# The last stage of a two-layer graph kernel: x1 of half of the rows added by TensorE into held PSUM tiles

## The chip, the cores and the metric

The kernel runs on one core of one Trainium2 chip. The metric is device time in microseconds (us), measured on the core. The kernel before takes 2655.48 us (median of three runs, 2652.28 to 2655.86). Its profiled execution has a span of 2651.3 us, and all moments given below are microseconds from the start of that span.

## What is computed

The input `x` has 16 images of 1024 rows and 256 channels, in float32. Layer 0 is a graph step with attention, a residual and a layer norm over the channels; it gives x1. Layer 1 aggregates x1 over a normalised adjacency matrix, then runs two linear layers, each followed by a batch norm over all 16 x 1024 rows, then adds x1 and takes a layer norm. Cut to the end of layer 1, with which this case deals:

```python
h   = relu(_batchnorm(x @ W1.T + b1, g1, be1))    # 512 features
out = _batchnorm(h @ W2.T + b2, g2, be2)          # 256 features
# and outside
x = _layernorm(x1 + out, axis=-1)                 # (x - mean) / sqrt(var + 1e-5)
```

The second batch norm needs the statistics of all 16 images before the first value of the result can be finished. So there is a point in the kernel at which everything waits for the last product of `h @ W2.T`, and a last stage behind it that passes over all images once more.

## The kernel before

The kernel is hand-scheduled: inside `tc.manual_schedule` TensorE (PE), ScalarE (ACT) and VectorE (DVE) each run their instructions in the order that the program writes them, apart from small moves that put an instruction ahead of another that would wait. GpSimd (POOL) computes small coefficient columns. All bulk transfers of the stage are issued from SyncE's queue (SP), in order.

The second linear layer (L1456) keeps its result transposed: for each image `b` a tile `o2T[b]` of 128 partitions with two halves `c` of 128 features, each with all 1024 rows in the free dimension. VectorE moves each half from PSUM with the bias added (L1460) and takes its batch norm statistics (L1464). All 16 `o2T` tiles stay in SBUF. After the last image `coefficients2` aggregates the statistics of a half (L1227), and GpSimd works out a scale `sg2` and a shift `sh2` for each feature (L1228 to L1231).

The last stage then runs, for each image:

- `scale_shift(b)`: two ACT passes of 128x1024, one for each half, that apply `sg2` and `sh2` in place (L1485).
- `residual2(b)`: TensorE turns `o2T[b]` back to rows, four 128x128 transposes into each of four PSUM tiles of 512 columns, one for each pair of row blocks (L1497). VectorE adds each PSUM tile to x1, which lies in SBUF as `xf[b]`, in place (L1502), and takes layer norm statistics of each 128x256 block, eight for an image (L1504). Ten small GpSimd operations turn these into `rstd` and `nmr`, the scale and the shift of each row (L1510 to L1519).
- `finish(b)`: eight ACT passes of 128x256 that write the normalised rows over `o2T[b]` (L1526), the store of the image (L1530), and the load of x1 for image `b + 7` (L1428) into the buffer that is now free. The x1 of the first three images is loaded while the linear layer still runs, that of the next four at the start of the stage.

The order in which these are written is `residual2(b)`, `scale_shift(b + 1)`, `finish(b - 1)`: on ACT the two passes for the next image stand ahead of the eight for the image before. The four PSUM tiles of an image come from two pools of two buffers.

Image 0's scale-and-shift for a half waits for that half's coefficients, and the second half's are the last to come.

Of the kernel before, what the change touches and what calls it, by code (L numbers as in the profile page):

```python
# [515 lines left out]
def fast_path(  # L516
# [34 lines left out]
    def open_psum():  # L551

        stack = ExitStack()
        for tag in "sto":
            psum[tag] = stack.enter_context(tc.tile_pool(name=f"ps_{tag}", bufs=2, space=PSUM))
        return stack
# [3 lines left out]
    def tile_s(name):  # L560
        return psum["s"].tile([P, N], F32, tag="s", name=name)

    def tile_t(name):
        return psum["t"].tile([P, HALF], F32, tag="t", name=name)

    def tile_o(name):
        return psum["o"].tile([P, HALF], F32, tag="o", name=name)
# [7 lines left out]
    ident = const.tile([P, P], F32, name="ident")  # L575
# [95 lines left out]
    H0, H1 = slice(0, HALF), slice(HALF, N)  # L671
# [3 lines left out]
    cols = {}  # L675
# [24 lines left out]
    with (  # L700
# [10 lines left out]
        st = {}  # L711
# [404 lines left out]
        with tc.manual_schedule(engines={mybir.EngineType.PE, mybir.EngineType.Activation, mybir.EngineType.DVE}):  # L1116
# [48 lines left out]
            for j in range(len(bursts)):  # L1165
                b, u = j // PERB, j % PERB
# [30 lines left out]
            j = len(bursts)  # L1197
# [14 lines left out]


    w1T, w2T = wl["w1T"], wl["w2T"]
    bn1_st = const.tile([P, HC, 2 * B, 6], F32, name="bn1_st")
    bn2_st = const.tile([P, CC, 2 * B, 6], F32, name="bn2_st")

    def batchnorm(stats, gamma, beta, k, name):

# [15 lines left out]
    with (  # L1235
# [9 lines left out]
        def bank(name):  # L1245
            return ps8.tile([P, HALF], F32, tag="bank", name=name)

        def temps(k):
            return lambda key, name: strt.tile([P, HALF], F32, tag=f"{key}{k}", name=f"{key}_{name}")


        wS = strt.tile([P, 4, C], F32, name="wS")
# [133 lines left out]
        def scale_shift1(h, k):  # L1386
            nc.scalar.activation(  # L1387
                h, h, AF.Relu, bias=sh1[:, k : k + 1], scale=sg1[:, k : k + 1]
            )
# [3 lines left out]
        for k in range(HC):  # L1393
            ps = [bank(f"ph_{k}_{half}") for half in range(2)]
            for c in range(CC):
                for half, hs in enumerate((H0, H1)):
                    nc.tensor.matmul(
                        ps[half], w1T[:, c, k * P : (k + 1) * P], t[:, c, hs],
                        start=(c == 0), stop=(c == CC - 1),
# [11 lines left out]
        nc.gpsimd.dma_start(h_d[B - 1], ht)  # L1411

    graph.close()
    ctx.enter_context(open_psum())

# [4 lines left out]
    with tc.tile_pool(name="o2p", bufs=1) as o2p:  # L1420
        o2T = [
            o2p.tile([P, CC, N], F32, tag=f"o2_{b}", name=f"o2_{b}") for b in range(B)
        ]
        xf = {}

        def load_x1(b, pool, tag):
            xf[b] = pool.tile([P, NCH, C], F32, tag=tag, name=f"xf_{b}")
            nc.sync.dma_start(xf[b], x1_d[b])  # L1428

        coefficients2, sg2, sh2 = batchnorm(bn2_st, cols["g2"], cols["be2"], CC, "bn2")  # L1430
        with (
            tc.tile_pool(name="hl", bufs=2) as hl,
            tc.manual_schedule(
                engines={mybir.EngineType.PE, mybir.EngineType.Activation, mybir.EngineType.DVE}
            ),
        ):
            hs_of = {0: h0}

            def load_h(b):
                ht = hl.tile([P, HC, N], F32, tag="hl", name=f"hl_{b}")  # L1440
                nc.sync.dma_start(ht, h_d[b])
                hs_of[b] = [ht[:, k, :] for k in range(HC)]

            load_h(1)
            for b in range(B):
                if b + 2 < B:
                    load_h(b + 2)
                if b + 1 < B:
                    for k in range(HC):
                        scale_shift1(hs_of[b + 1][k], k)  # L1450
                h = hs_of.pop(b)
                for c in range(CC):
                    ps = tile_s(f"po2_{b}_{c}")
                    for k in range(HC):
                        for hs in (H0, H1):
                            nc.tensor.matmul(  # L1456
                                ps[:, hs], w2T[:, k, c * P : (c + 1) * P], h[k][:, hs],
                                start=(k == 0), stop=(k == HC - 1),
                            )
                    nc.vector.tensor_scalar(  # L1460
                        o2T[b][:, c, :], ps, cols["b2"][:, c : c + 1], None, ALU.add
                    )
                    for half, hs in enumerate((H0, H1)):
                        nc.vector.bn_stats(bn2_st[:, c, 2 * b + half, :], o2T[b][:, c, hs])  # L1464
                    if b == B - 1:
                        coefficients2(c)
                if b >= B - 3:
                    load_x1(b - (B - 3), xp, "x")

        with (
            tc.tile_pool(name="fin2", bufs=4) as fin2,
            tc.manual_schedule(
                engines={mybir.EngineType.PE, mybir.EngineType.Activation, mybir.EngineType.DVE}
            ),
        ):
            for b in range(3, 7):
                load_x1(b, fin2, "xf")  # L1480

            def scale_shift(b):
                for c in range(CC):
                    o = o2T[b][:, c, :]
                    nc.scalar.activation(  # L1485
                        o, o, AF.Identity, bias=sh2[:, c : c + 1], scale=sg2[:, c : c + 1]
                    )

            def residual2(b):
                xt = xf[b]  # L1490
                st = small.tile([P, NCH, 6], F32, tag="ln_st", name=f"st_l1_{b}")
                for pair in range(NCH // 2):
                    pt = tile_t(f"pf_{b}_{pair}") if pair % 2 else tile_o(f"pf_{b}_{pair}")
                    for j in range(2):
                        n = 2 * pair + j
                        for c in range(CC):
                            nc.tensor.transpose(  # L1497
                                pt[:, j * C + c * P : j * C + (c + 1) * P],
                                o2T[b][:, c, n * P : (n + 1) * P], ident,
                            )  # L1500
                    xs = xt[:, 2 * pair : 2 * pair + 2, :].rearrange("p n c -> p (n c)")
                    nc.vector.tensor_add(xs, pt, xs)  # L1502
                    for n in (2 * pair, 2 * pair + 1):
                        nc.vector.bn_stats(st[:, n, :], xt[:, n, :])  # L1504

                me, qe, mo, qo = (st[:, :, k] for k in (1, 2, 4, 5))
                w = small.tile([P, 4, NCH], F32, tag="ln_w", name=f"w_l1_{b}")
                rstd, nmr, dif, var = (w[:, k, :] for k in range(4))
                pool = nc.gpsimd
                pool.tensor_tensor(nmr, me, mo, ALU.add)  # L1510
                pool.tensor_tensor(dif, me, mo, ALU.subtract)
                pool.tensor_tensor(var, qe, qo, ALU.add)
                pool.tensor_scalar(var, var, 1.0 / C, EPS, ALU.mult, ALU.add)
                pool.tensor_tensor(dif, dif, dif, ALU.mult)
                pool.tensor_scalar(dif, dif, 0.25, None, ALU.mult)
                pool.tensor_tensor(var, var, dif, ALU.add)
                pool.tensor_tensor(rstd, var, mhalf, ALU.pow)
                pool.tensor_tensor(nmr, nmr, rstd, ALU.mult)
                pool.tensor_scalar(nmr, nmr, -0.5, None, ALU.mult)  # L1519
                return rstd, nmr  # L1520

            def finish(b, rstd, nmr):
                xt = xf.pop(b)
                y = o2T[b].rearrange("p c n -> p (c n)").rearrange("p (n c) -> p n c", c=C)
                for n in range(NCH):
                    nc.scalar.activation(  # L1526
                        y[:, n, :], xt[:, n, :], AF.Identity,
                        bias=nmr[:, n : n + 1], scale=rstd[:, n : n + 1],
                    )
                nc.sync.dma_start(out[b].rearrange("(n p) c -> p n c", p=P), y)  # L1530
                if b + 7 < B:
                    load_x1(b + 7, *((fin2, "xf") if 3 <= b < 7 else (xp, "x")))

            scale_shift(0)
            coeffs = {}
            for b in range(B):
                coeffs[b] = residual2(b)
                if b + 1 < B:
                    scale_shift(b + 1)
                if b:  # L1540
                    finish(b - 1, *coeffs.pop(b - 1))
            finish(B - 1, *coeffs.pop(B - 1))


# [41 lines left out]
```

## Time and profile before

| what | value |
|---|---|
| time | 2655.48 us |
| span of the profiled execution | 2651.3 us |
| TensorE busy over the span | 96% |
| last product of the second linear layer | ends at 2531.7 |
| first normalising pass of the last stage | starts at 2549.07 |
| last normalising pass | ends at 2644.28 |
| ACT busy, 2560 to 2580 | 20.00 of 20.00 us |
| VectorE busy in the same stretch | 17.77 |
| TensorE busy in the same stretch, and its granted clock | 11.39, 0.56 |

How to read the profile's lines: a table by stage gives for each stretch its length and then, engine by engine, the busy time and the number of instructions in brackets; PEld is TensorE's loading of weights, which overlaps its products. PEclk is the granted clock of TensorE as a share of full speed, then come the busy share of the 16 DMA engines and what they moved. A line of the timeline has the start, the duration of the merged group, the engine, the source line, the operation, its tiles and shapes and the number of instructions. In square brackets stands how long the engine had been idle before and which instruction ended the wait.

### The profile page before, as it was taken

What the parts mean: (1) busy time and instruction counts of PE and PEld (TensorE: products, weight loads), DVE (VectorE), ACT (ScalarE), POOL (GpSimd) and SP (SyncE); (2) the same over time, 40 slices, a digit from 0 to 9 for tenths busy, and PEclk for the clock granted to TensorE, in tenths of its full rate; (3) what the DMA queues carried; (4) which work ended last, traced back from release to release, by engine and by line L of the source; (5) the groups of instructions that cost most, each with busy time, mean ns of one, the idle gap of its engine ahead of it and who ended that gap; (6) DMA issues with size and microseconds to landing.
All of it is one profiled execution on the core that took longest, in us unless ns stands there. A gap on an engine that the chain in (4) does not pass through costs nothing. (4 is left out here: it accounts for less than half of the span.)

```text
span 2651.3 us, 31994 instructions
## 1 busy us (share of the span) xinstructions
PE 2553.7 (96%) x12966; PEld 1110.1 (42%) x12966; DVE 1600.2 (60%) x2160; ACT 1126.8 (43%) x1349; POOL 336.2 (13%) x407
## 2 busy tenths in 40 slices
PE   8999999999999999999999999999999999999964
PEld 4443444444434434444444343344444444444443
DVE  5465665756656657666566576765655655533376
ACT  5363563654645636545446354410101001233368
POOL 0001000100100011001000100321222211100044
PEclk9999999999999999999999999999999999999975
DMA  4001101001011011010110110112122122353367
GB/s 143 2 9 41 33 10 41 21 22 33 9 41 33 9 41 33 10 41 3 39 33 9 41 49 1 41 64 95 80 95 95 66 92 82 137 202 143 149 222 240
DMA packets 134557, 168.94 MB, mean 64 GB/s; under 512 B 86785, under 2 KB 120065, under 8 KB 124033
## 3 DMA queue, kind: packets, MB, share of 16 engines
q1 hardware_dynamic: 129568, 116.47, 14.2%
q0 software_dynamic: 4832, 50.34, 4.6%
q8 instruction: 103, 1.69, 0.3%
q14 instruction: 54, 0.43, 0.0%
HBM read 99.36 MB, written 67.44 MB: 63 GB/s over the span
## 5 line engine op out<-in xcount | busy, mean ns | idle before, releaser
L908 ACT ACTIVATE p<-ps 128x1024 f32<-128x1024 f32 x512 | 495.7, 1020 | 179.5 <-PE ps L903 142.9
L933 DVE TENSOR_TENSOR acc<-acc,p 128x1024 f32<-128x1024 f32 x384 | 483.2, 1258 | 61.0 <-ACT p L908 32.4
L903 PE MATMUL ps<-qT,kT 64*64 64x512 f32 x4096 | 490.6, 594 | 1.4 <-ACT p L908 1.4
L924 PE MATMUL po<-p,v 64*64 64x512 f32 x4096 | 485.3, 589 | 0.0
L805 PE MATMUL pg<-wg,x 128*128 128x512 f32 x960 | 425.2, 596 | 0.0
L979 POOL TENSOR_TENSOR x<-x,o 128x512 f32<-128x512 f32 x64 | 109.5, 1711 | 1434.8 <-DVE o L974 1434.8
L924 PEld LDWEIGHTS po<-p,v 64*64 64x64 f32 x4096 | 156.7, 133 | 282.8 <-issue 282.6
L805 PEld LDWEIGHTS pg<-wg,x 128*128 128x128 f32 x960 | 177.6, 190 | 226.9 <-issue 203.3
L903 PEld LDWEIGHTS ps<-qT,kT 64*64 64x64 f32 x4096 | 146.1, 132 | 280.2 <-issue 231.5
L817 ACT ACTIVATE qT<-qT 128x512 f32<-128x512 f32 x64 | 40.3, 631 | 482.0 <-DVE qT L814 481.9
L1456 PE MATMUL po<-hl,w12T 128*128 128x512 f32 x512 | 220.3, 592 | 3.1 <-ACT hl L1387 2.3
L814 DVE SCALAR_TENSOR_TENSOR qT<-pg,para_s 128x512 f32<-128x512 f32 x64 | 43.9, 689 | 271.1 <-PE pg L805 269.8
L793 DVE SCALAR_TENSOR_TENSOR wg<-wg,adj_s 128x1024 f32<-128x1024 f32 x128 | 153.1, 1217 | 15.5 <-ACT wg L789 15.5
L784 ACT ACTIVATE wg<-crow,ccol 128x1024 f32<-128x1024 f32 x128 | 146.6, 1146 | 11.8 <-DMA crow<-c 11.8
L1456 PEld LDWEIGHTS po<-hl,w12T 128*128 128x128 f32 x512 | 97.1, 190 | 126.3 <-issue 120.5
L789 ACT ACTIVATE wg<-wg 128x1024 f32<-128x1024 f32 x128 | 135.5, 1060 | 2.6
L1387 ACT ACTIVATE hl<-hl,bn_sh,bn_sg 128x1024 f32<-128x1024 f32 x64 | 74.3, 1229 | 135.0 <-DMA hl<-h 133.6
L855 PE MATMUL pv<-kvw_s,xT 128*128 128x256 f32 x512 | 124.0, 385 | 1.6 <-ACT kT L846 1.6
L1460 DVE TENSOR_SCALAR o<-po,col_b 128x1024 f32<-128x1024 f32 x32 | 41.1, 1284 | 139.1 <-PE po L1456 139.1
L842 PE MATMUL pk<-xT,kvw_s 128*128 128x512 f32 x256 | 120.3, 592 | 0.0
L855 PEld LDWEIGHTS pv<-kvw_s,xT 128*128 128x128 f32 x512 | 94.9, 190 | 51.9 <-issue 27.6
L1286 PE MATMUL a_agg<-ahT,x1l 128*128 128x512 f32 x240 | 108.1, 593 | 1.1 <-ACT agg L1104 1.1
(151 smaller groups left out, 2625.4 us busy)
## 6 DMA issues: line engine op xcount, KB each, us to landing
h<-hw POOLq DMA_DIRECT2D x16, 2048.0 KB, 6.6
hl<-h SPq DMA_DIRECT2D x15, 2048.0 KB
x<-x POOLq DMA_DIRECT2D x16, 1024.0 KB, 4.2
x1l<-x SPq DMA_DIRECT2D x16, 1024.0 KB
xf<-x SPq DMA_DIRECT2D x16, 1024.0 KB
out_dram<-o SPq DMA_DIRECT2D x16, 1024.0 KB
x<-in_x_dram SPq DMA_DIRECT2D x15, 1024.0 KB
crow<-c SPq DMA_DIRECT2D x15, 512.0 KB
```

The source lines that it names most:

```text
L784: nc.scalar.activation(w, s["crow"], AF.Abs, bias=s["ccol"][:, n : n + 1])
L789: nc.scalar.activation(w, w, AF.Tanh, scale=0.5)
L793: nc.vector.scalar_tensor_tensor(w, w, 1.0, adj_s[:, n, :], op0=ALU.subtract, op1=ALU.mult)
L805: nc.tensor.matmul(ps, xt[:, n, c * P : (c + 1) * P], s["wg", n][:, hs], start=(n == 0), stop=(n == NCH - 1),)
L842: nc.tensor.matmul(ps, kvw_s[:, c, kc * P : (kc + 1) * P], s["xT"][:, c, hs], start=(c == 0), stop=(c == CC - 1),)
L855: nc.tensor.matmul(pt[:, j * C : (j + 1) * C], s["xT"][:, c, n * P : (n + 1) * P], kvw_s[:, c, C : 2 * C], start=(c == 0), stop=(c == CC - 1),
L903: nc.tensor.matmul(ps[kh * D : (kh + 1) * D, hd * HALF : (hd + 1) * HALF], kT[r, pr, ks], qT[r, pr, qh * HALF : (qh + 1) * HALF], start=Tr ...
L908: nc.scalar.activation(p, ps, AF.Exp)
L924: nc.tensor.matmul(g["po"][kh][hd * D : (hd + 1) * D, :], s["v"][r, m, h * D : (h + 1) * D], p[r, hd * HALF : (hd + 1) * HALF], start=(m = ...
L933: nc.vector.tensor_add(g["acc"], g["acc"], p)
L979: nc.gpsimd.tensor_tensor(xs, xs, o.rearrange("p n h d -> p n (h d)"), ALU.add)
L1456: nc.tensor.matmul(ps[:, hs], w2T[:, k, c * P : (c + 1) * P], h[k][:, hs], start=(k == 0), stop=(k == HC - 1),)
```

## The change

The change takes work off ACT and VectorE in the last stage and gives some of it to TensorE.

- The second half of an image's rows (pairs 2 and 3) is no longer added on VectorE. TensorE multiplies the identity with x1's rows into a PSUM tile of 1024 columns, `held[b]` (`add_x1`), and then accumulates onto it the products of `o2T[b]` with the identity, which are the transposed rows. VectorE takes the statistics of the four blocks straight from the held tile, after all of the image's products, and ACT's normalising passes read it there. `held` has three tiles[...]; the transposes of pairs 0 and 1 have two tiles of one bank each. For that the PSUM pools of the linear layer are closed first.
- Of the eight normalising passes ACT keeps six; the first two blocks go to VectorE (`tensor_scalar`), behind the next image's statistics in its order.
- The bias of the very last half of the linear layer is added by ACT, in two halves of 512 columns, instead of by VectorE in one, and image 0's scale-and-shift is cut in halves of 512 as well, so that the stage can begin sooner.
- The tiles for batch norm statistics move to pools that end with their stage.

```diff
-    bn1_st = const.tile([P, HC, 2 * B, 6], F32, name="bn1_st")
-    bn2_st = const.tile([P, CC, 2 * B, 6], F32, name="bn2_st")
...
+        bn1_st = strt.tile([P, HC, 2 * B, 6], F32, name="bn1_st")
...
+        bn2_st = o2p.tile([P, CC, 2 * B, 6], F32, name="bn2_st")
...
-                    nc.vector.tensor_scalar(
-                        o2T[b][:, c, :], ps, cols["b2"][:, c : c + 1], None, ALU.add
-                    )
+                    if b == B - 1 and c == CC - 1:
+                        for hs in (H0, H1):
+                            nc.scalar.activation(
+                                o2T[b][:, c, hs], ps[:, hs], AF.Identity,
+                                bias=cols["b2"][:, c : c + 1],
+                            )
+                    else:
...
+        part_psum.close()
         with (
             tc.tile_pool(name="fin2", bufs=4) as fin2,
+            tc.tile_pool(name="ps_held", bufs=3, space=PSUM) as ps_held,
+            tc.tile_pool(name="ps_sum", bufs=2, space=PSUM) as ps_sum,
...
+                for hs in (H0, H1) if b == 0 else (slice(0, N),):
+                    for c in range(CC):
+                        o = o2T[b][:, c, hs]
...
+            def add_x1(b, pair):
+                if b not in held:
+                    held[b] = ps_held.tile([P, N], F32, tag="held", name=f"held_{b}")
+                nc.tensor.matmul(
+                    held[b][:, (pair - 2) * HALF : (pair - 1) * HALF], ident,
+                    xf[b][:, 2 * pair : 2 * pair + 2, :].rearrange("p n c -> p (n c)"),
+                    start=True, stop=False, skip_group_check=True,
+                )
...
-                for pair in range(NCH // 2):
-                    pt = tile_t(f"pf_{b}_{pair}") if pair % 2 else tile_o(f"pf_{b}_{pair}")
+                for pair in range(2):
+                    pt = ps_sum.tile([P, HALF], F32, tag="sum", name=f"pf_{b}_{pair}")
...
+                for pair in range(2, 4):
+                    if b:
+                        add_x1(b, pair)
+                    pt = held[b][:, (pair - 2) * HALF : (pair - 1) * HALF]
+                    for j in range(2):
+                        n = 2 * pair + j
+                        for c in range(CC):
+                            nc.tensor.matmul(
+                                pt[:, j * C + c * P : j * C + (c + 1) * P],
+                                o2T[b][:, c, n * P : (n + 1) * P], ident,
+                                start=False, stop=True, skip_group_check=True,
+                            )
+                for n in range(4, NCH):
+                    nc.vector.bn_stats(st[:, n, :], held[b][:, (n - 4) * C : (n - 3) * C])
...
-                for n in range(NCH):
+                for n in (0, 1):
+                    nc.vector.tensor_scalar(
+                        y[:, n, :], xt[:, n, :], rstd[:, n : n + 1], nmr[:, n : n + 1],
+                        ALU.mult, ALU.add,
+                    )
+                for n in (4, 5, 6, 7, 2, 3):
                     nc.scalar.activation(
-                        y[:, n, :], xt[:, n, :], AF.Identity,
-                        bias=nmr[:, n : n + 1], scale=rstd[:, n : n + 1],
+                        y[:, n, :], hx[:, (n - 4) * C : (n - 3) * C] if n >= 4 else xt[:, n, :],
+                        AF.Identity, bias=nmr[:, n : n + 1], scale=rstd[:, n : n + 1],
                     )
...
+            add_x1(0, 2)
+            add_x1(0, 3)
             scale_shift(0)
```

More of the change, by code (lines that the diff above doesn't have):

```diff
@@ L1413, in fast_path @@
     graph.close()
-    ctx.enter_context(open_psum())
+    part_psum = open_psum()
     with tc.tile_pool(name="o2p", bufs=1) as o2p:
@@ L1459, in fast_path @@
                             )
-                    nc.vector.tensor_scalar(
-                        o2T[b][:, c, :], ps, cols["b2"][:, c : c + 1], None, ALU.add
-                    )
+                    if b == B - 1 and c == CC - 1:
[6 more added lines that the diff above has]
+                        nc.vector.tensor_scalar(
+                            o2T[b][:, c, :], ps, cols["b2"][:, c : c + 1], None, ALU.add
+                        )
                     for half, hs in enumerate((H0, H1)):
@@ L1482, in scale_shift @@
             def scale_shift(b):
[L1483 to L1487, printed above, removed]
+                for hs in (H0, H1) if b == 0 else (slice(0, N),):
+                    for c in range(CC):
+                        o = o2T[b][:, c, hs]
+                        nc.scalar.activation(
+                            o, o, AF.Identity, bias=sh2[:, c : c + 1], scale=sg2[:, c : c + 1]
+                        )
+            held = {}
+            def add_x1(b, pair):
[6 more added lines that the diff above has]
+                )
             def residual2(b):
@@ L1504, in residual2 @@
                         nc.vector.bn_stats(st[:, n, :], xt[:, n, :])
+                for pair in range(2, 4):
[9 more added lines that the diff above has]
+                                start=False, stop=True, skip_group_check=True,
+                            )
+                for n in range(4, NCH):
+                    nc.vector.bn_stats(st[:, n, :], held[b][:, (n - 4) * C : (n - 3) * C])
                 me, qe, mo, qo = (st[:, :, k] for k in (1, 2, 4, 5))
@@ L1522, in finish @@
             def finish(b, rstd, nmr):
-                xt = xf.pop(b)
+                xt, hx = xf.pop(b), held.pop(b)
                 y = o2T[b].rearrange("p c n -> p (c n)").rearrange("p (n c) -> p n c", c=C)
-                for n in range(NCH):
+                for n in (0, 1):
+                    nc.vector.tensor_scalar(
+                        y[:, n, :], xt[:, n, :], rstd[:, n : n + 1], nmr[:, n : n + 1],
+                        ALU.mult, ALU.add,
+                    )
+                for n in (4, 5, 6, 7, 2, 3):
                     nc.scalar.activation(
-                        y[:, n, :], xt[:, n, :], AF.Identity,
-                        bias=nmr[:, n : n + 1], scale=rstd[:, n : n + 1],
+                        y[:, n, :], hx[:, (n - 4) * C : (n - 3) * C] if n >= 4 else xt[:, n, :],
+                        AF.Identity, bias=nmr[:, n : n + 1], scale=rstd[:, n : n + 1],
                     )
```

## The prediction

> **What bounds the kernel now.** The page's slices show TensorE at 9 tenths until the last two or three and then at 6 and 4: only the end is not TensorE's. The change lies there, so I read the table of busy time by stage.
>
> ```profile
> core 0: us, PE busy (x) PEld busy (x) DVE busy (x) ACT busy (x) POOL busy (x), PEclk, DMA share, GB/s
> 2555.00:2560.00 5.00, 3.46 (x15) 3.06 (x15) 4.46 (x11) 5.00 (x10) 3.41 (x10) 0.60 1.03 348
> 2580.00:2585.00 5.00, 3.16 (x15) 2.92 (x15) 4.26 (x10) 5.00 (x10) 3.44 (x10) 0.71 1.03 341
> 2605.00:2610.00 5.00, 3.46 (x15) 3.06 (x15) 4.32 (x11) 5.00 (x10) 3.44 (x10) 0.50 1.02 338
> 2610.00:2615.00 5.00, 3.94 (x16) 3.25 (x16) 4.31 (x10) 5.00 (x10) 2.83 (x8) 0.50 0.60 209
> ```
>
> ScalarE (ACT) is busy for all of every stretch; VectorE for 4.3 to 4.5 of 5, TensorE for 3.2 to 3.9 at a clock near one half. The DMA engines are full too until 2613. Next, the order of events over one of the 16 images:
>
> ```profile
> 2586.27 4.03 ACT L1526 ACTIVATE o<-xf,w_l 128x256 f32<-128x256 f32 x8
> 2586.42 3.46 PE L1497 MATMUL pf<-ident,o 128*128 128x128 f32 x15 [0.80 <-ACT o L1485]
> 2587.05 0.21 POOL L1510 TENSOR_TENSOR w_l<-st_l 128x8 f32<-128x8 f32 x1 [2.32 <-DVE st_l L1504]
> 2588.88 0.67 DVE L1502 TENSOR_TENSOR xf<-pf,xf 128x512 f32<-128x512 f32 x1
> 2589.59 0.75 DVE L1504 BATCH_NORM_STATS2 st_l<-xf 128x6 f32<-128x256 f32 x2
> 2590.21 2.36 ACT L1485 ACTIVATE o<-o,bn_sh,bn_sg 128x1024 f32<-128x1024 f32 x2
> 2590.25 0.67 DVE L1502 TENSOR_TENSOR xf<-pf,xf 128x512 f32<-128x512 f32 x1
> 2590.75 0.24 POOL L1519 TENSOR_SCALAR w_l<-w_l 128x8 f32<-128x8 f32 x1
> 2592.47 4.03 ACT L1526 ACTIVATE o<-xf,w_l 128x256 f32<-128x256 f32 x8
> ```
>
> ACT's eight normalising passes start at 2586.27, its two scale-and-shift passes at 2590.21, the next eight at 2592.47: 3.94 + 2.26 = 6.20 us an image, with no gap. So a pass costs 0.4925 (3.94/8). VectorE needs 1.37 for an add and two statistics (2588.88 to 2590.25), 5.5 an image: second. GpSimd's ten small operations last 3.94 (2587.05 to 2590.99). Last, the two ends of the stage:
>
> ```profile
> 2531.69 1.28 DVE L1460 TENSOR_SCALAR o<-po,col_b 128x1024 f32<-128x1024 f32 x1 [3.21 <-PE po L1456]
> 2537.15 5.77 ACT L1485 ACTIVATE o<-o,bn_sh,bn_sg 128x1024 f32<-128x1024 f32 x5 [5.63 <-POOL bn_sh L1231]
> 2549.07 4.04 ACT L1526 ACTIVATE o<-xf,w_l 128x256 f32<-128x256 f32 x8 [6.15 <-POOL w_l L1519]
> 2640.24 4.04 ACT L1526 ACTIVATE o<-xf,w_l 128x256 f32<-128x256 f32 x8 [2.03 <-POOL w_l L1519]
> ```
>
> Here ACT waits: for the coefficients of the batch norm, for the first image's statistics, for the last image's. It ends at 2644.28; the last store lands at 2651.3, 7.0 later.
>
> [...] (1) [...] 1-us stretches show 0.50 or 1.00, and full came at 2542, 3.5 us after products began at 2538.45. (2) [...] with transposes alone the clock fell to 0.50 at 2549 although TensorE was about half busy in the 5 us before. (3) [...] Here VectorE's add from PSUM takes 677 (L1502) against 683 to 691 for adds in SBUF[...]. (4) [...] The trace has the weight load of a transpose at 137 ns at best, of a plain product (L1456) at 190.
>
> **The change part by part.**
>
> *ACT.* Eight passes become six (two go to VectorE): 2.26 + 6 x 0.4925 = 5.21 us an image[...]. That is 1.0 off the bounding engine.
>
> *VectorE.* Two of four adds go; two passes of 128x256 come. The same form runs earlier (L600): eight in 2.67 us, so 0.325 apart. Sum: 2 x 1.37 + 4 x 0.335 (statistics from PSUM) + 2 x 0.325 = 4.73[...]. Below ACT either way. The two passes stand behind the next image's statistics in VectorE's order, so they run at about the time of ACT's six for the same image; the store waits for both, and ACT's are the later.
>
> *TensorE.* Eight of 16 transposes become plain products onto x1, and two 128x512 products with the identity come. None of this is in the trace as it stands, so I bound it. Half clock: transposes (3.46 - 0.48)/14 = 0.213 apart; plain ones 0.31 (an estimate: 0.213 plus twice the 53 ns of the longer weight load); the 128x512 twice the 0.43 at which L1456's products follow each other: 8 x 0.213 + 8 x 0.31 + 2 x 0.86 = 5.9. Full clock: 0.108 for a transpose (four at L970 in 0.60), about 0.17 for a plain one, 0.43: 3.1. I take 4.6, a mixture: at half clock TensorE would be busy without a gap, which by (1) brings full clock[...].
>
> *The wait.* The statistics of the held half wait for all 18 products, and everything behind them on VectorE with them. In time: from the end of an image's scale-and-shift, 0.1 + 4.6 (products) + 0.2 + 1.44 (four statistics at 0.36) + 0.1 + 3.95 (GpSimd) = 10.4. Between that end and this image's finish ACT has two finishes and two scale-and-shifts to do, 2 x 5.21 = 10.4. So the chain just fits; period 5.25. The three held tiles add no wait: a tile is read out about 13 us after its scale-and-shift and asked for again at three periods, 15.75, plus the first products. The two transposes' buffers (four before) are freed by adds of the image before.
>
> *Start.* ACT adds the last bias in two halves, the first of them already while the last product runs; at 0.69 each (L1404, the same form) the second ends at 2532.5, its statistics at 2533.2 against 2534.30: 1.1 gained, coefficients at 2536.05. Then a half pass of 0.80 (between 0.585 for 256 and 1.226 for 1024 elements), so TensorE starts at 2536.85 (2538.45 before). Its first 16 products at half clock end at 2541.1, statistics at 2542.8, GpSimd at 2546.8: first finish at 2546.8, against 2549.07. The two x1 products of image 0 run while the coefficients are awaited: nothing.
>
> *End.* Finish of image 13, before which the last scale-and-shift ends: 2546.8 + 13 x 5.25 = 2615.05. Chain 10.4, then six passes 2.95: 2628.4, against 2644.28: 15.9 less. The store's 7.0 stays.
>
> *Statistics tiles moved to other pools.* Nothing in the loops before changes its order; the first write of o2 waits in addition for an aggregate that VectorE has itself just done: nothing.
>
> **Forecast:** 2655.48 - 15.9 = 2639.6.
>
> **Rivals.**
>
> A: TensorE stays at half clock and becomes the bound. For: the 0.50 above. Against: (1), and that it would have no gaps. Period 5.9: 2546.8 + 76.7 + 0.1 + 5.9 + 1.64 + 4.05 + 2.95 = 2638.1, 6.2 less: 2649.3.
>
> B: the DMA engines bind. For: ten stores and nine loads filled the DMA engines from 2554 to 2613 at a share of 1.0, 6.2 us for each pair, just ACT's period: with 5.25 they fall 0.95 behind an image, 8.6 over nine. Against: x1 of an image is asked for seven images ahead, some 23 us before its use, and after that only stores remain, about 3.2 us each, so the lag is made up before the last. If it bound for nine images: gained are 2.2 at the start, 6 x 0.95 later, 1.3 at the end, 9.2: 2646.3.
>
> C: slower. The plain products cost as much as their weight loads doubled, 0.38, the transposes 0.23 and the wide ones 0.95 at half clock: 6.8 an image, with all statistics behind them. The first finish would end at 2536.85 + 1.84 + 3.04 + 1.64 + 4.05 + 2.95 = 2550.4, the last fifteen periods later, 2652.4, 8.1 after the present end: 2663.6. Against: no gapless stretch of TensorE stays at half clock for more than about 4 us in this trace.
>
> **How the numbers follow.** Forecast 0.75, A 0.12, B 0.08, C 0.05. [...] With B inside and A and C left out, 2634.5 to 2647.5 holds 0.83. Under 2650.2 (0.2%) lie the forecast, B and most of A: faster 0.89; within 0.2% 0.05; slower 0.06.
>
> **What would show it.** ACT still without gaps at 5.2 us an image, with six passes; the clock above 0.8 between 2555 and 2615; the four PSUM statistics at about 0.42 each, starting less than 0.3 after the last product; first finish near 2546.8. Wrong would be: ACT idle before its first finish pass of each image (chain or TensorE too long), TensorE without gaps at 0.50, or products waiting for x1 from DMA.

## The result, and the profile after

The changed kernel takes 2637.39 us (median of four runs, 2633.17 to 2638.31) against 2655.16 us of the kernel before on the same chip. The ratio is 0.9932, with a 95% interval of 0.9915 to 0.9949: 17.8 us less, where 15.9 were forecast.

The profiled execution of after has a span of 2635.9 us. Before looking at the stage one has to know where it begins. The last product of the linear layer ends at 2533.95 in this trace and ended at 2531.7 in that of before; in a second trace of the unchanged kernel after it ends at 2530.3. So this moment moves by some 3.7 us from run to run, and single spans can't be compared to a microsecond. Below, the parts of the stage are counted **from the last product**:

| from the last product's end | before | after |
|---|---|---|
| first normalising pass on ACT starts | 17.4 | 14.6 |
| mean period of an image, ACT | 6.20 | 5.14 |
| last normalising pass on ACT ends | 112.6 | 94.7 |
| end of the span | 119.6 | 101.9 |

The second trace of the kernel after has the same period, 5.14, but its first pass starts at 16.1 and its last ends at 96.2; why, is taken up below.

The table by stage of the kernel after, for the same stretches as were shown of before:

```profile
core 0: us, PE busy (x) PEld busy (x) DVE busy (x) ACT busy (x) POOL busy (x), PEclk, DMA share, GB/s
2555.00:2560.00 5.00, 4.52 (x29) 3.40 (x28) 4.10 (x12) 5.00 (x9) 3.02 (x8) 1.00 1.01 349
2580.00:2585.00 5.00, 4.27 (x28) 3.08 (x26) 4.70 (x13) 5.00 (x10) 3.62 (x10) 1.00 1.06 409
2605.00:2610.00 5.00, 4.60 (x28) 3.40 (x28) 4.68 (x13) 5.00 (x9) 3.37 (x9) 1.00 0.65 220
2610.00:2615.00 5.00, 4.60 (x28) 3.40 (x28) 4.70 (x13) 4.85 (x9) 3.54 (x10) 1.00 0.58 193
```

ACT is still the engine without gaps, nearly: 4.85 of 5 in the last line. TensorE and VectorE stand close under it, at 4.1 to 4.7 of 5. The clock is 1.00 throughout; it was 0.50 to 0.71. The column of instructions has a surprise: TensorE executes 28 or 29 in 5 us, although the program has 18 products for an image.

Next, the timeline of one image of after:

```profile
2584.53 1.93 ACT L1570 ACTIVATE o<-held,w_l 128x256 f32<-128x256 f32 x4
2585.49 1.02 PE L1508 MATMUL held<-xf,ident 128*128 128x512 f32 x2
2586.34 1.09 ACT L1570 ACTIVATE o<-xf,w_l 128x256 f32<-128x256 f32 x2
2586.35 1.05 PE L1537 MATMUL held<-ident,o 128*128 128x128 f32 x8
2587.24 1.02 PE L1508 MATMUL held<-xf,ident 128*128 128x512 f32 x2
2587.32 2.37 ACT L1499 ACTIVATE o<-o,bn_sh,bn_sg 128x1024 f32<-128x1024 f32 x2
2588.10 1.05 PE L1537 MATMUL held<-ident,o 128*128 128x128 f32 x8
2589.19 1.42 DVE L1543 BATCH_NORM_STATS2 st_l<-held 128x6 f32<-128x256 f32 x4 [0.50 <-PE held L1537]
2589.58 1.92 ACT L1570 ACTIVATE o<-held,w_l 128x256 f32<-128x256 f32 x4
2590.53 0.72 DVE L1565 TENSOR_SCALAR o<-xf,w_l 128x256 f32<-128x256 f32 x2
```

ACT's image is 2584.53 to 2589.58, 5.05: four passes from the held tile (1.81, so 0.4525 each), two from SBUF (0.98, 0.49 each), two scale-and-shifts (2.26). TensorE's four groups between 2585.49 and 2588.99 show the held half: a wide product is one call in the program and two instructions in the trace, 0.86 us from start to start; a group of four 128x128 products is eight instructions in 0.89. VectorE waits 0.50 for the last of them, then takes four statistics in 1.42.

Before every third image ACT waits a little, and it waits at the start and at the end. The waits of ACT and VectorE in the stage (total, times, longest), and the lines of the two ends:

```profile
ACT o L1570 <- POOL w_l L1558: 8.2, 7, 3.0
DVE st_l L1543 <- PE held L1537: 5.4, 14, 0.8
```

```profile
2533.99 1.26 ACT L1463 ACTIVATE o<-po,col_b 128x512 f32<-128x512 f32 x2 [0.59 <-PE po L1457]
2535.30 1.98 PE L1508 MATMUL held<-xf,ident 128*128 128x512 f32 x4 [1.36 <-ACT o L1463]
2538.85 6.75 ACT L1499 ACTIVATE o<-o,bn_sh,bn_sg 128x512 f32<-128x512 f32 x7 [3.60 <-POOL bn_sh L1229]
2548.55 1.93 ACT L1570 ACTIVATE o<-held,w_l 128x256 f32<-128x256 f32 x4 [2.95 <-POOL w_l L1558]
2625.79 1.93 ACT L1570 ACTIVATE o<-held,w_l 128x256 f32<-128x256 f32 x4 [2.41 <-POOL w_l L1558]
```

Of ACT's 8.2 us of waits 2.95 come before the first finish; the second-to-last and the last finish wait 2.15 and 2.41, and the other four, 0.15 to 0.17 each, are the small waits. The first of the two bias halves starts at 2533.99, 0.04 after the last product ends, and the second follows it; none ran beside that product.

### The profile page after: what moved, and what is told of

Same layout as the page of the kernel before. It is cut to its first block, busy times and chain, and to the rows that moved or that the text cites. A ratio compares the mean times of both kernels' runs of the same rounds, so it can differ in the third digit from the quotient of the medians.

```text
span 2635.9 us, 32325 instructions
## 1 busy us (share of the span) xinstructions
PE 2572.7 (98%) x13158; PEld 1118.6 (42%) x13158; DVE 1587.8 (60%) x2159; ACT 1110.2 (42%) x1321; POOL 338.9 (13%) x407
## 3 DMA queue, kind: packets, MB, share of 16 engines
q8 instruction: 105, 1.72, 0.3%
## 5 line engine op out<-in xcount | busy, mean ns | idle before, releaser
L1457 PE MATMUL po<-hl,w12T 128*128 128x512 f32 x512 | 222.0, 596 | 3.6 <-ACT hl L1387 2.8
L1457 PEld LDWEIGHTS po<-hl,w12T 128*128 128x128 f32 x512 | 97.7, 191 | 127.9 <-issue 120.4
L1286 PE MATMUL b_agg<-aT,x1S 128*128 128x512 f32 x240 | 109.2, 598 | 0.0
```

Of the source, the lines that this page charges most:

```text
L1286: nc.tensor.matmul(ps, left, right, start=(start and i == 0), stop=(i == NCH // 2 - 1), skip_group_check=True,)
L1457: nc.tensor.matmul(ps[:, hs], w2T[:, k, c * P : (c + 1) * P], h[k][:, hs], start=(k == 0), stop=(k == HC - 1),)
```

## The experiments

Theory 1 was the forecast's: ACT bounds the stage, and taking 1.0 us of passes off it is what moves the period, while the adds on TensorE make the room on VectorE that this needs. The rivals: that TensorE's clock does it; that the early start does it; that the DMA engines take part in the limit. Each part was first done or undone alone.

**All eight passes back on ACT.** The kernel after, without VectorE's two passes:

```diff
-for n in (0, 1):
-    nc.vector.tensor_scalar(...)
-for n in (4, 5, 6, 7, 2, 3):
+for n in (4, 5, 6, 7, 0, 1, 2, 3):
     nc.scalar.activation(...)
```

> The changed kernel, but with all eight normalising passes of an image on ScalarE again (VectorE none); everything else as changed. Theory 1 (ScalarE's number of passes sets the period): 2.26 + 4 x 0.4525 + 4 x 0.4925 = 6.04 us an image instead of 5.14, no idle time on ScalarE; over 13 periods 11.7 and 0.9 more at the end: about 2650. Rival (what counted was VectorE's relief from two adds, or TensorE's faster clock): period stays near 5.2 and the time near 2638 to 2640.

Measured: 2649.73 us, ratio 0.9981 (0.9974 to 0.9989). ACT's timeline in this kernel:

```profile
2591.07 1.99 ACT L1565 ACTIVATE o<-held,w_l 128x256 f32<-128x256 f32 x4
2597.10 2.00 ACT L1565 ACTIVATE o<-held,w_l 128x256 f32<-128x256 f32 x4
```

A period of 6.03 with no wait of ACT, at a clock of 1.00. So 12 of the 18 us hang on the two passes: the periods alone are 13 x (6.03 - 5.14) = 11.6. Of the 5 that remain without them, 13 x (6.20 - 6.03) = 2.2 are in the periods, where each of the four passes from the held tile takes 0.45 and one from SBUF 0.49, and 1.3 at the start, where the first finish comes 16.1 after the last product. A full clock with ACT at eight passes moves the period no further.

**Only the passes moved, in the kernel before.** The same two passes given to VectorE, with its four adds an image left as they were:

```diff
-for n in range(NCH):
+for n in (0, 1):
+    nc.vector.tensor_scalar(...)
+for n in (4, 5, 6, 7, 2, 3):
     nc.scalar.activation(...)
```

> The kernel before, with one part of the change alone: the first two normalising passes of each image on VectorE, no held tiles. Theory 1 with VectorE as the next limit: ScalarE needs 2.26 + 6 x 0.4925 = 5.21, but VectorE 4 x 1.375 + 2 x 0.325 = 6.15, so the period goes from 6.20 to 6.15 only and ScalarE shows idle time; with about 1 at the end the time is near 2653.5. Rival (the passes alone are the gain, and VectorE has room): period 5.2 to 5.5, time 2641 to 2645.

Measured: 2654.31 us, ratio 1.0001 (0.9993 to 1.001). ACT's timeline, then the busy time of ten microseconds (columns as above):

```profile
2593.19 3.06 ACT L1531 ACTIVATE o<-xf,w_l 128x256 f32<-128x256 f32 x6 [0.83 <-POOL w_l L1519]
2599.35 2.07 ACT L1531 ACTIVATE o<-xf,w_l 128x256 f32<-128x256 f32 x4 [0.83 <-POOL w_l L1519]
```

```profile
2580.00:2590.00 10.00, 7.11 (x31) 6.18 (x31) 9.79 (x23) 8.32 (x15) 5.17 (x17) 0.55 1.02 333
```

ACT has its smaller work but waits 0.83 before each image, and VectorE is busy 9.79 of 10: the period stays at 6.16. ACT's relief is worth nothing until VectorE loses two adds, which this change gives to TensorE; and the experiment before shows that without ACT's relief most of the gain is missing. The two parts pay together.

**Only the clock.** The kernel before with its sixteen transposes an image written as plain products:

```diff
-nc.tensor.transpose(pt[...], o2T[b][...], ident)
+nc.tensor.matmul(pt[...], o2T[b][...], ident, start=True, stop=True, ...)
```

> The kernel before, with the sixteen transposes of an image written as plain products with the identity; nothing else. Theory 1: the period stays 6.20 (ScalarE is the limit), time within 2 us of before. On the clock: [...] if it is only that TensorE is busy for a larger share in the changed kernel (4.5 of 5 against 3.4 of 5), the clock stays at 0.5 to 0.7. Rival to theory 1 (half clock held up the stage): period clearly under 6.2 and time 3 us or more under before.

Measured: 2656.2 us, ratio 1.0006 (0.9999 to 1.0013). From 2560 to 2615 TensorE is busy 40.52 of 55 us at a mean clock of 0.93, in the kernel before 33.45 at 0.58, but ACT's period stayed at 6.20 and ACT was busy 55.00 of 55.00 us there. The first finish came 18.5 after the last product, later than before. A higher clock alone is worth nothing in this stage. It didn't make the products faster: in the kernel after a plain product of 128 columns takes 0.22 us at full clock, twice a transpose's 0.108, and a transpose at half clock takes 0.213 in the kernel before. That a TensorE with less work would not help the kernel before either is read from ACT, which had no gap.

**Only the start.** The kernel before with the bias halves on ACT and image 0's scale-and-shift in halves:

```diff
+if b == B - 1 and c == CC - 1:
+    for hs in (H0, H1):
+        nc.scalar.activation(o2T[b][:, c, hs], ps[:, hs], ..., bias=...)
...
-for c in range(CC):
+for hs in (H0, H1) if b == 0 else (slice(0, N),):
+    for c in range(CC):
```

> The kernel before, with the start part of the change alone: the last bias on ScalarE in two halves, and the first image's scale-and-shift in halves. From the end of the last product to the first normalising pass it took 17.4 us before and 14.6 in the changed kernel. Theory: this part alone gives the 1.1 of the statistics and 0.45 of the half pass, 1.5: 15.9 us, period 6.20 as before, time near 2653.6. Rival: the whole 2.8 comes from it, time near 2652.3; the other rival: none of it, as ScalarE's extra bias passes only move the wait.

Measured: 2653.59 us, ratio 0.9997 (0.9989 to 1.0006). By the trace the first finish is 16.4 after the last product, 1.0 less than before. That is the size of it; a ratio can't tell it from nothing.

**Held tiles in halves.** The kernel after with each `held` tile of 1024 columns cut into two of 512, one for each pair, so that the statistics of pair 2 wait for pair 2 only:

```diff
-held[b] = ps_held.tile([P, N], F32, tag="held", ...)       # bufs=3
+held[b, pair] = ps_held.tile([P, HALF], F32, tag="held", ...)  # bufs=6
...
```

> The changed kernel, with each held tile of two PSUM banks cut into two of one bank, so that the statistics of pair 2 wait for pair 2's products alone and not for all of the image's. Theory: the wait behind all products is nearly hidden. The chain from scale-and-shift to finish, 10.3 us in the changed kernel, gets about 0.6 shorter, ScalarE loses its small waits before every second image (period 5.14 to 5.05) and 0.6 at the end: 1.8 in all, near 2635.6. Rival (the wait is a main cost of the changed kernel): 5 us or more under it. Other rival (VectorE, at 4.7 of 5, is the true limit): no gain at all.

Measured: 2635.32 us, ratio 0.9926 (0.9911 to 0.9941). The small waits of ACT are gone and the period is 5.04, so "the statistics wait for all products" cost what the mean period of 5.144 has over 5.05, about 0.1 an image. The median lies 2 us under the kernel after and the intervals overlap, so the time alone doesn't show it. Counted from the last product, the last ACT pass ends at 93.7, against 94.7 and 96.2 in the two traces of the kernel after.

**Without the x1 products.** The kernel after with TensorE's wide products left out, so that half of the rows are normalised without x1:

```diff
-if b:
-    add_x1(b, pair)
+if b not in held:
+    held[b] = ps_held.tile([P, N], F32, ...)
...
-start=False, stop=True, ...
+start=True, stop=True, ...
...
-add_x1(0, 2)
-add_x1(0, 3)
```

> The changed kernel without the products of the identity with x1 (the second half of the rows is then normalised without x1): TensorE has the eight transposes and eight plain products of an image alone, 2.6 us at full clock instead of 4.3. Theory (ScalarE sets the period at 5.05, TensorE has room): period 5.05, chain 1.7 shorter at the end and about that at the start if the clock holds, 2634 or so. The clock stays above 0.8 if plain products hold it up. Rival (TensorE, busy 4.5 of 5, limits the changed kernel): period 4.8 or less is impossible for ScalarE, but all its waits would be gone and the gain 3 us or more. Clock rival: without the wide products it falls to 0.5 to 0.7 as before, and the time comes out near 2637.

Measured: 2638.18 us, ratio 0.9936 (0.992 to 0.9951). Taking 1.7 us of work an image off TensorE gains nothing; the 2634 of the theory didn't come. The clock is 0.84 from 2570 to 2590 instead of 1.00, TensorE is busy 14.79 of those 20 us, and ACT 19.90. So TensorE does not bound the steady state of the kernel after: with less work its clock is lower, and ACT goes on without a wait. At the start the variant loses: without the early products image 0's transposes run at half clock, and the first finish comes 16.5 after the last product.

**Image 0's x1 products not early.** They are moved from the wait for the coefficients to where all other images have them:

```diff
-if b:
-    add_x1(b, pair)
+add_x1(b, pair)
...
-add_x1(0, 2)
-add_x1(0, 3)
```

> The changed kernel with image 0's two products of x1 moved from ahead of the coefficients to behind image 0's transposes. In the changed kernel TensorE's clock stays at full while it waits for the coefficients; before, it fell to half at 3.5 us after the last product. Theory: the early products keep the array's clock up; without them image 0's products run at half clock, transposes 0.213 and plain products about 0.35 each, wide ones 1.72, and the first normalising pass comes 3 to 6 us later after the last product than 14.6. As ScalarE has no slack later, the time goes up by as much: near 2641. Rival: only their own 1.7 us at full clock matter, 2639; or nothing, as GpSimd's chain sets the first pass.

Measured: 2647.55 us, ratio 0.9969 (0.9956 to 0.9982), about 10 us over the kernel after and much more than expected. Image 0's products run at half clock (0.50 from 2540 to 2545), and the first finish comes 18.2 after the last product instead of 14.6. But 3.6 is not 10: the rest is lost later, where ACT waits 1.85 before every third image and 4.77 before the last.

**The early products back, the later order kept.** To tell whether the early burst holds the clock or the order matters, both were put in: image 0's x1 products early and, overwriting them, once more at the later place.

```diff
 # the kernel of the experiment above, and
+add_x1(0, 2)
+add_x1(0, 3)
 scale_shift(0)
```

> The kernel after with the two early x1 products of image 0 kept in the wait for the coefficients, and computed once more at the later place where the slower variant (products not early) had them; the later ones overwrite the early ones. So the order of all work that counts is that variant's, and only the early burst on TensorE is back. Theory clock (the early burst keeps TensorE at full clock, and that alone is worth the 10 us): about 2639 us, within 2 of the kernel after plus the 1.7 us of TensorE's doubled work in image 0; clock 1.00 in the steady state. Rival, order (the place of the x1 products ahead of the coefficients matters, because it shortens image 0's chain and fixes the phase of the images): about 2647 us, as without the early products, with half clock in stretches.

Measured: 2646.87 us (eleven runs), ratio 0.9969 (0.996 to 0.9978): the figure of the rival, order. Six runs lie at 2646.9 to 2648.0, four at 2643.3 to 2644.0, one at 2637.63. The trace says more than the median. Image 0 ran at a clock of 1.00, so the burst did what I had credited it with, and the first finish came at 15.8. The loss comes later. TensorE's and ACT's timelines of this kernel, then two stretches in a row, with the granted clock in the third column from the right:

```profile
2554.41 0.33 PE L1522 MATMUL pf<-ident,o 128*128 128x128 f32 x1 [0.88 <-ACT o L1499]
2555.54 0.98 PE L1522 MATMUL pf<-ident,o 128*128 128x128 f32 x7 [0.80 <-ACT o L1499]
2556.36 1.68 PE L1508 MATMUL held<-xf,ident 128*128 128x512 f32 x2
2557.84 1.91 PE L1536 MATMUL held<-ident,o 128*128 128x128 f32 x8
```

```profile
2567.45 1.93 ACT L1569 ACTIVATE o<-held,w_l 128x256 f32<-128x256 f32 x4 [1.85 <-POOL w_l L1557]
2584.56 1.93 ACT L1569 ACTIVATE o<-held,w_l 128x256 f32<-128x256 f32 x4 [1.84 <-POOL w_l L1557]
2601.67 1.93 ACT L1569 ACTIVATE o<-held,w_l 128x256 f32<-128x256 f32 x4 [1.84 <-POOL w_l L1557]
```

```profile
2553.18:2556.60 3.42, 1.74 (x13) 1.32 (x12) 3.25 (x10) 3.42 (x6) 2.61 (x8) 1.00 0.72 232
2556.60:2560.01 3.41, 3.41 (x11) 2.37 (x10) 2.31 (x6) 3.41 (x6) 2.59 (x6) 0.50 1.03 325
```

This is a **cycle that feeds itself**. TensorE has run ahead and idles 0.88 and 0.80 (with one product between) for ACT's scale-and-shift. Then its clock falls to half for 3.41 us, from 2556.60 to 2560.01, and the eight products that take 1.05 take 1.91. ACT then waits 1.85 for that image's statistics, its next scale-and-shift is as much later, TensorE idles for it again (1.09 and 0.80 before 2572.66), and so on every 17.1 us: three images at 5.70 instead of 5.05. In the kernel after TensorE's longest idle time is 0.73 from 2560 on, and the cycle doesn't begin.

What goes before it can be read from the traces, which record the granted clock. In all 14 of them it changes, from the end of the linear layer on, only at moments that are whole multiples of 3.41 us apart: in that of before at 2535.15, 2541.98, 2548.81, 2559.05 and 2562.46, for example. Where these moments lie differs from run to run. Cut along them, the time until TensorE's last product gives 386 stretches, each wholly at 1.00 or wholly at 0.50, and the clock of a stretch goes with TensorE's busy time in the stretch before it. After a stretch at full clock with more than 1.74 us busy the next was always at full clock (239 stretches), and with less than 1.57 always at half (46); in between both occur. After a stretch at half clock, more than 2.76 us busy always brought full clock (44) and less than 2.70 never did (43). This is a relation found in the traces, in this stage alone; no run was made to test it.

By this relation it isn't the length of a gap that counts but how much of one stretch is idle. The 2.32 us of idle before image 0's products agree with it: they are followed by full clock in the first trace of the kernel after and by half clock in the second.

```profile
2535.33:2538.74 3.41, 2.07 (x5) 0.79 (x5) 1.68 (x3) 0.00 (x0) 1.28 (x5) 1.00 0.93 368
2538.74:2542.16 3.42, 2.24 (x18) 2.05 (x19) 1.83 (x4) 3.31 (x5) 0.07 (x1) 1.00 1.02 434
```

```profile
2534.10:2537.51 3.41, 1.26 (x10) 1.08 (x10) 0.85 (x2) 2.33 (x4) 0.81 (x4) 1.00 1.03 430
2537.51:2540.92 3.41, 3.41 (x16) 3.41 (x17) 2.04 (x6) 3.41 (x4) 0.00 (x0) 0.50 1.01 425
```

In the first trace (upper lines) the gap, 2537.39 to 2539.72, is shared by two stretches, which are 2.07 and 2.24 busy; in the second all but 0.4 us of it lies in one stretch, which is only 1.26 busy. The idle times of 0.88 and 0.80 that open the cycle here lie in one stretch, 1.74 busy. The same two in the kernel without late loads (below) lie on both sides of a boundary, the stretches are 2.47 and 2.69 busy, and no half clock follows. And since the cycle's 17.1 us are five times 3.41, the gap meets nearly the same place of a stretch each time.

The run at 2637.63 was without the cycle, by its mean granted clock: 0.997 over the whole kernel, where the other ten have 0.993 or 0.994 and the kernel after has 0.996 to 0.998.

**Without the late loads.** The kernel after, with no load of x1 from image 7 on; those images take the x1 of the image seven before them:

```diff
-load_x1(b + 7, ...)
+xf[b + 7] = xt
```

> The kernel after without the loads of x1 from image 7 on (those images take the tile of the image seven before, so x1 in their sums is wrong data, which changes no duration). Theory (DMA is hidden): the same time within 1.5 us, 2637.4, with the DMA share well below 1 in the steady state. Rival B (DMA takes part in the limit): up to 2 us faster, by finish passes or transposes that no longer wait.

The kernel after was run again beside it:

> The kernel after, unchanged, as the yardstick of this comparison. 2637.4 us, ratio 0.993, TensorE at a clock of 1.00 throughout the last stage.

Measured: 2636.67 us without the loads, ratio 0.9934 (0.9919 to 0.995), and 2638.33 us for the kernel after, ratio 0.9941 (0.9928 to 0.9955), which here is 14.4 us less than the kernel before; the forecast's 15.9 lies between this and the 17.8 of the result. One stretch of the kernel without loads:

```profile
2580.00:2585.00 5.00, 4.60 (x28) 3.40 (x28) 4.70 (x13) 4.85 (x8) 3.55 (x11) 1.00 0.55 186
```

The DMA share falls from 1.06 to 0.55. ACT is busy 19.79 us from 2560 to 2580, with the loads 19.67, and the time is the same. The loads are hidden. The stores could not be taken away.

**Two versions meant to be better.** The first has the held halves, nine GpSimd operations instead of ten in each image's chain, and the last image's passes split four and four between VectorE and ACT, its store in two halves:

```diff
-pool.tensor_tensor(nmr, me, mo, ALU.add)
-pool.tensor_tensor(dif, me, mo, ALU.subtract)
+pool.tensor_tensor(var, me, mo, ALU.add)
+pool.tensor_scalar(nmr, var, -0.5, None, ALU.mult)
+pool.tensor_tensor(dif, me, nmr, ALU.add)
...
-pool.tensor_scalar(dif, dif, 0.25, None, ALU.mult)
...
-pool.tensor_scalar(nmr, nmr, -0.5, None, ALU.mult)
...
-for n in (0, 1):
+for n in (0, 1) if b < B - 1 else (0, 1, 2, 3):
...
```

> The changed kernel with three things more: held halves as in the run before; GpSimd's chain of ten operations cut to nine (0.28 us); and for the last image four normalising passes each on VectorE and ScalarE, stored in two halves. Theory: 1.2 from the period (5.14 to 5.05), 0.9 from the shorter chain at the end, 1.0 from four passes instead of six, about 1.6 from a last store of half the size: 4.7, near 2632.7. Rival (the store's 7 us are latency, not size): 3.1, near 2634.3.

Measured: 2636.9 us, ratio 0.993 (0.9917 to 0.9944); the expectation missed by 4. By its trace the last ACT pass ended 92.2 after the last product, against 94.7 and 96.2 in the two traces of the kernel after; image 0's products ran at half clock here, as in the second of these. The halved last store gave nothing: from the last ACT pass to the end of the span it is 7.5 us, after 7.2, as the rival of this expectation had it. Why the median shows only 0.5 us of the rest is open; the two kernels were not run side by side.

The second, because image 0's products ran at half clock in that trace, moves image 1's two x1 products ahead of the coefficients as well, so that TensorE idles 0.61 instead of 2.32 before image 0's transposes:

```diff
-if b:
+if b > 1:
     add_x1(b, pair)
...
-add_x1(0, 2)
-add_x1(0, 3)
+for early in (0, 1):
+    add_x1(early, 2)
+    add_x1(early, 3)
```

> The variant with held halves, the shorter GpSimd chain and the split last image, with image 1's two x1 products moved ahead of the coefficients as well, so that TensorE idles about 0.6 us instead of 2.3 before the first transposes. Theory clock: no half-clock episode at 2541 to 2545 (the held halves and the improved variant lost 1.5 us to one), image 1's chain 1.7 us shorter; first finish at +13.6 after the last product, period 5.04, 2635.0 us or a little less, ratio 0.992. Rival[...]: it stays, and the time is 2636.9 as before.

Measured: 2634.69 us, ratio 0.9924 (0.991 to 0.9937), 3.6 us under the kernel after in the same comparison, with five runs each that hardly overlap (2630.97 to 2635.15 against 2634.8 to 2638.86). Image 0's half clock is gone, as expected. The first finish, at 14.4, is 0.8 later than expected, and one half-clock episode came at 2553.5, after idle times of 1.79 and 0.80. The stretch before it, with most of both idle times in it, was 1.21 busy. The episode cost ACT 0.86 once and didn't repeat. That the shorter chain has slack to swallow such an episode fits the kernel without x1 products too, where one stretch in three is at half clock and ACT is still busy 19.90 of 20 us; neither run tests the slack alone. This version has the lowest median of those run, but it isn't shown to be better than the first: the intervals overlap, and its last ACT pass ended 92.5 after the last product, the first one's at 92.2.

## Why the prediction was right, and where it was not

The forecast was 2639.6, and the stage was to end its last pass 96.7 after the last product. It ended at 94.7 in the first trace and at 96.2 in the second. The 2.0 us in the first divide into 0.5 at the start, 13 x (5.25 - 5.144) = 1.4 in the periods and 0.1 at the end.

- **ACT's term held.** 5.21 was worked out, and 5.05 is what an image takes without waits: a pass from the held tile takes 0.4525, one from SBUF 0.4925. The trace of before didn't show this, as none of the stage's ACT passes there reads PSUM, and the forecast has one price for all six. The difference is 13 x (5.21 - 5.05) = 2.1 us by the passes alone, of which the small waits leave 1.4.
- **VectorE's term held.** In the trace of after, statistics from the held tile take 414 ns in the median, from SBUF 419. VectorE is busy 50.86 of 55 us, 4.76 an image, where 4.73 was worked out.
- **TensorE's term was right by luck.** I took 4.6, my estimate of a mixture between 3.1 at full and 5.9 at half clock. The clock was full, and 4.36 is the sum that the trace gives: two wide products at 0.86, eight plain ones at 0.22 (0.89 for four), eight transposes at 0.108. Here the wide and plain terms were mis-sized: 0.43 and 0.17 stood for what are 0.86 and 0.22. I read 0.43 off the products of the linear layer without counting them: the trace there too has two instructions to each product that the program writes (512 for 256). And the clock went with transposes as with plain products. In the kernel before 16 transposes filled a stretch at half clock, from 2538.57 to 2541.98, and full clock followed; 14 were busy for 2.22 us of the next, and it stayed. The fall at 2548.81, which stands under (2) in the prediction, followed a stretch that was 1.69 busy, and with plain products the clock fell after one of 1.72 (in the variant with late x1 products). What plain products change is the amount: 16 of them are 16 x 0.22 = 3.5 us an image at full clock, 16 transposes 1.7.
- **Rival A was mis-sized in the same way.** In the variant with late x1 products a wide product takes 1.71 from start to start at half clock, a group of four plain ones as long, a transpose 0.22: 8.6 an image, not 5.9. (The prediction's 0.31 for a plain product is 0.32 by its own sum, which is small beside this.) A half clock that lasts would have made the change slower than before, by an estimate from these figures. What carried the prediction is that a TensorE without gaps didn't stay at half clock, and that half of the argument held: in the variants with the cycle each half clock ended after a single stretch of 3.41 us. What it left out is that full clock was lost again where TensorE idled for about half of such a stretch (1.74 of 3.41 busy, the first time). With the cycle and the later start the stage was 9.5 and 12.0 us longer than in the first trace of the kernel after.
- **The chain just fits, as forecast.** 10.3 against two periods of 10.1 makes the waits of 0.16 before every third image. What I didn't see is that in a chain with no slack a single half-clock episode can bring on the next.
- **The start: two steps failed and offset each other.** The bias on ACT was to begin 0.43 before the last product ends. Even the first half, whose own products are done earlier, started 0.04 after the tile's last product, and the coefficients came 0.5 later than forecast. And "the two x1 products of image 0: nothing" was wrong: in the trace of after the clock stays at 1.00 over image 0's products, which took 3.2 us and not the 4.25 taken, and so the first finish came 0.5 sooner. In the second trace of the same kernel image 0's products fell to half clock and the first finish came at 16.1, a microsecond later than the forecast's 15.1, so this gain of up to 1.5 us isn't sure. There the last pass ended within 0.5 of the forecast, because a late start and a short period offset each other.
- **The end held:** 13.3 from the start of image 13's finish to the last pass's end, where 13.35 was worked out.
- **Rival B fell.** The DMA share reached 1.06 and nothing waited for it; without the late loads, half of that traffic, the time is the same.

## What to carry to other kernels

When three engines stand close together, relief for the first is worth only as much as the second has room for: add up the next engine's work before moving anything to it, as the passes alone, at a ratio of 1.0001, show. Count the instructions of a product in the trace before using its interval as its price. And where TensorE is only just fast enough, look at its busy time over stretches of a few microseconds and not at the mean: in this stage a stretch of 3.41 us that was idle for about half was followed by half clock, the lower clock made the next gap, and that loop took most of some 10 us.

## What was not expected of the hardware

- A plain float32 product shows as two matmul instructions with a weight load each (L1457: 512 of either for 256 products). At full clock it takes 0.86 us for 512 columns, 0.22 for 128. A float32 transpose shows as one, 0.108.
- A DMA share of 1.0 was no limit here: the same stage moved 338 to 348 GB/s at 1.02 to 1.03 before and 409 GB/s at 1.06 after.
- In this stage of the 14 traces the clock changed only at moments whole multiples of 3.41 us apart, and it went with TensorE's busy time in the stretch before: from full to half after less than about 1.6 to 1.7 us, from half to full after more than about 2.7 to 2.8. With transposes alone, in the kernel before, it fell after 1.69 at most and rose after 2.76 at least.
